# Where the row maxima of an attention are taken: a different share between the feed-forward and the heads, in a fused macaron block

## The chip, the cores and the metric

The kernel runs on one core of one Trainium2 chip. It is one launch that computes the whole block. Times are device microseconds (us) of the core. Five engines work beside each other, each through its own queue in order: TensorE (PE; its weight loads are PEld), VectorE (DVE), ScalarE (ACT), GpSimd (POOL) and SyncE (SP, which issues most of the DMAs). TensorE writes its results to PSUM, which has eight banks of 512 float32 values for each of 128 partitions.

## The reference

The input x has 4 sequences of 1024 rows of 512 values. A feed-forward, an attention and the same feed-forward again are added to it:

```python
x = x + 0.5 * ffn(layernorm(x), w_gate_up, w_proj)
x = x + attn(layernorm(x), Wq, bq, Wk, bk, Wv, bv, Wo, bo)
x = x + 0.5 * ffn(layernorm(x), w_gate_up, w_proj)

def ffn(x, w_gate_up, w_proj):            # weights made ternary in groups of 64, H = 2048
    gate, up = split(x @ quant(w_gate_up).T)
    h = silu(gate) * up
    return rms_norm(h) @ quant(w_proj).T

def attn(x, ...):                          # 32 query heads on 8 key heads, 16 wide
    Q, K, V = rope(x @ Wq.T + bq), rope(x @ Wk.T + bk), x @ Wv.T + bv
    w = softmax(Q @ K.T / 4)               # over 1024 keys
    return (w @ V) @ Wo.T + bo
```

## The kernel before

**Stages.** After the weights are quantised (together with the first two blocks of feed-forward), the program runs, for each of the four sequences b: a feed-forward stage (`FeedForward.run`, three blocks of 512 rows, so 48 units of 128 hidden values each), the heads of the attention (`Attention.run`), and a stage that ends this attention and projects the next sequence's Q, K and V. A last feed-forward stage of two blocks ends the kernel. In each of these loops the order of the instructions on every engine is the order in which the program writes them.

**A unit of the feed-forward.** `hidden` makes gate and up for 512 rows (16 matmuls of tile gu, L205), Silu on ScalarE, the product h on VectorE (L217), the square of h on POOL (sq, L225) summed into acc (L229). `project` (L245, tile po) follows two units later (LAG). At the end of a block, `sums` (L258, tile pq) adds the squares over the partitions with matmuls against ones, and `factors` turns them into half the inverse root: ms on VectorE (L273), inv on POOL (L98), half on VectorE (L277). `end` (x, L288) then scales po and adds it to x. At the end of a stage two units are left to project, tile by tile of 128 rows, and `factors` is called behind the second of the four tiles.

**The maxima.** The softmax needs the largest score of every row before its exps, since it subtracts it. The scores are therefore made twice. `maxima` makes them once in a form of two terms (matmul of tile sm, L1162: 128 rows against 512 keys, contracted over 64 of the 128 rows of the array, the lower half for even heads j and the upper half for odd ones) and VectorE reduces them to one column of pm (TENSOR_REDUCE, L1171). A sequence has 512 of them: 8 groups of 4 heads (G), each with 16 items (ITEMS: 8 row tiles, two halves of the keys). When a group, or from group 6 on half a group, is complete, `subtract_maxima` makes its negated maxima into rows: three short operations on VectorE (L1219 to L1223), a transposition on TensorE (pmT, L1201, in a bank of sm) and a copy (mrow, L1203). The rows of groups 0 to 2 go through DRAM (d_m, L1206) and come back on POOL's queue (`maxima_in`, L1242); those of later groups go by SP (L1213). They lie in even_rows or odd_rows.

**Where the maxima are taken.** `early` is called in each unit of the feed-forward and puts four maxima there, between two projections, as long as a share of EARLY is not yet reached and the unit is not one of a few left out. The rest comes in the heads.

**The heads.** 128 steps per sequence: for each group g and half of the queries qh, eight steps kc of 128 keys. One step makes the scores of two pairs of heads (`scores`, tile s, L1293, two matmuls a pair, one in each half of the array's rows), the exps (e, L1302, ScalarE), and, one step later, their product with the values (`weigh`, tile o, L1309, eight matmuls). The scores of a step are added to those of the step before in the same PSUM tile (the keys are stored as differences), so s of step kc must wait for the exps of kc - 1 of its pair; the maxima are subtracted once, in the first step of every eight, by two further matmuls a pair against the rows (L1293 too, `s<-even_rows,pick`). At the end of eight steps ScalarE copies o out (oT, L1318). PSUM holds two s tiles of two banks, three banks of sm (`bufs=3`) and one of o. Before the change a step takes three maxima, two behind the first pair's scores and one behind the second's, by a pattern of heads written out by hand; step 0 takes none. All matmuls of a step are written first, and the exps and reduces behind them.

**Key places.** `Places` holds the tiles of queries and keys for maxima ("m") and scores ("s") in four slots, and loads the next when an older one is over.

Of the kernel before, what the change touches and what calls it, by code (L numbers as in the profile page):

```python
# [10 lines left out]
F32 = mybir.dt.float32  # L11
BF16 = mybir.dt.bfloat16
F32R = mybir.dt.float32r
AF = mybir.ActivationFunctionType
# [8 lines left out]
HQ, HKV, HD = 32, 8, 16  # L23
G = HQ // HKV
# [13 lines left out]
def tile_macaron_block(  # L38
# [17 lines left out]
    nc = tc.nc  # L56
# [78 lines left out]
    class FeedForward:  # L135
# [176 lines left out]
        def chunks(self):  # L312
            last = len(self.order) - 1
            due, ends = [], []
            for n, (k, hc) in enumerate(self.order):
                if self.beside is not None and n > 0:
                    places.piece()
                parts, rest = self.hidden(k, hc)
                if ends:
                    self.end(*ends.pop(), [2, 3])  # L320
                due.append((k, hc, parts))
                behind = due.pop(0) if len(due) > self.LAG else None
                if behind is not None:
                    self.project(*behind, [0, 1])
                if n == last:
                    rest()
                if self.beside is not None:
                    share = (n - self.begin) / (last - 1 - self.begin)
                    self.beside(self.ps, share, n < last and (k == 0 or hc != self.LAG - 1))
                if behind is not None:  # L330
                    self.project(*behind, [2, 3])
                    if behind[1] == HC - 1:
                        half = self.factors(behind[0])
                        self.end(behind[0], half, [0, 1])
                        ends.append((behind[0], half))
                if n < last:
                    rest()
                if k + 1 < len(self.blocks) and 4 <= hc < 12 and hc % 2 == 0:
                    for turn in self.normalize(k + 1, [hc // 2 - 2], self.wp, self.ps, "gu"):
                        self.later.append((hc + 1, turn))  # L340
                for step in [step for step in self.later if step[0] == hc]:
                    self.later.remove(step)
                    step[1]()

            if len(self.accs[k]) > 1:
                self.sums(k, 0)
            for i in range(4):
                for behind in due:
                    self.project(*behind, [i])
                if i == 1:  # L350
                    half = self.factors(k)
            self.end(k, half)
            for _, step in self.later:
                step()
# [348 lines left out]
    class Places:  # L703
# [33 lines left out]
        def rest(self):  # L737
            while self.pieces:
                self.piece()
# [171 lines left out]
    class Attention:  # L911
# [17 lines left out]
        ITEMS = NT * 2  # L929
        TOTAL = HKV * ITEMS * G  # L930
        FIRST = 3
        EARLY = (3 * ITEMS - 4) * G

        def __init__(self, b):
            self.b = b
# [308 lines left out]
        def early(self, ps, share, more):  # L1244
# [12 lines left out]
            if self.turning:  # L1257
                self.turning.pop(0)()
            if more and sum(self.counts) + G <= min(share, 1.0) * self.EARLY:
                ends = [self.maxima(sum(self.counts) % G, ps, 4) for _ in range(G)]  # L1260
# [10 lines left out]
        def run(self, keep, wp, ps):  # L1271
            b = self.b
            o = None
            self.wp, self.ps = wp, ps
            self.odd_rows = wp.tile([P, T], F32R, tag="rows", name=f"odd_rows_{b}", bufs=1)

            sums = {}

            def scores(g, qh, kc, pair):

                name = f"{b}_{g}_{qh}_{kc}_{pair}"
                keys, queries = slice(kc * P, (kc + 1) * P), slice(qh * 512, (qh + 1) * 512)
                *q, k = places.at["s", b, g]
                if kc == 0:
                    sums[pair] = ps.tile([P, 2, 512], F32, tag="s", name=f"s_{b}_{g}_{qh}_{pair}", bufs=2)
                s = sums[pair]
                terms = [(k[:, keys], q[pair])]
                if kc == 0:
                    terms.append((pick[:, pair, :], self.mrows[g]))
                for n, (lhsT, rhs) in enumerate(terms):  # L1290
                    for e in range(2):
                        at = slice(e * PAIR, (e + 1) * PAIR)
                        nc.tensor.matmul(  # L1293
                            s[:, e, :],
                            lhsT=lhsT[at],
                            rhs=rhs[at, queries],
                            start=(kc == 0 and n == 0),
                            stop=(n == len(terms) - 1),
                            skip_group_check=True,
                        )  # L1300
                w = wp.tile([P, 2, 512], F32, tag="e", name=f"e_{name}", bufs=4)
                return w, lambda: nc.scalar.activation(w, s, AF.Exp, scale=1.0 / HD**0.5)  # L1302

            def weigh(g, qh, kc, es):
                nonlocal o
                if kc == 0:
                    o = ps.tile([P, 512], F32, tag="o", name=f"o_{b}_{g}_{qh}")
                for j in range(G):
                    nc.tensor.matmul(  # L1309
                        o[j * SLOT : (j + 1) * SLOT, :],  # L1310
                        lhsT=vs[:, kc, g, :],
                        rhs=es[j // 2][:, j % 2, :],
                        start=(kc == 0),
                        stop=(kc == NT - 1),
                    )
                if kc == NT - 1:
                    oT = wp.tile([P, 512], F32, tag="oT", name=f"oT_{b}_{g}_{qh}")
                    nc.scalar.copy(oT, o)  # L1318
                    nc.sync.dma_start(
                        self.d_o[g * G : (g + 1) * G, :, :, qh * 512 : (qh + 1) * 512].rearrange(  # L1320
                            "j r d t -> (j r d) t"
                        ),
                        oT,
                    )
                    if qh == NB - 1 and g % 2 == 1:
                        self.divide(g // 2, keep)
                        self.when = n


            pattern = [((0, 1), (2,)), ((3, 0), (1,)), ((2, 3), (0,)), ((1, 2), (3,))]  # L1330
            late = None
            places.load(("t2", b + 1) if b + 1 < B else ("out", B))
            for n in range(HKV * self.STEPS):
                g, qh, kc = n // self.STEPS, n // NT % NB, n % NT
                if n % self.STEPS == 4 and g > 0:
                    places.done(("s", b, g - 1))
                if n % self.STEPS > 0 and g + 1 < HKV and g + 1 in self.mT and g + 1 not in self.mrows:
                    self.maxima_in(g + 1)
                if self.after and n in (self.when + 7, self.when + 12, self.when + 15):
                    self.after.pop(0)()  # L1340
                if n == HKV * self.STEPS - 8 and b + 1 < B:
                    at[b + 1].rows_ahead(keep)
                turn = self.turning.pop(0) if self.turning else None
                sides = pattern[n % 4] if n > 0 else [(), ()]
                es, ends = {}, []
                for pair, heads in enumerate(sides):
                    es[pair], end = scores(g, qh, kc, pair)
                    ends.append(end)
                    for j in heads:
                        if self.counts[j] < HKV * self.ITEMS:  # L1350
                            ends.append(self.maxima(j, ps, 3))
                for end in ends:
                    end()
                if self.chores:
                    self.chores.pop(0)()
                if late is not None:
                    weigh(*late)
                if turn is not None:
                    turn()
                if n == 0:  # L1360
                    nc.gpsimd.memset(self.odd_rows.bitcast(F32), 0.0)
                late = g, qh, kc, es
            weigh(*late)
            places.done(("s", b, HKV - 2))
            places.done(("s", b, HKV - 1))
# [31 lines left out]
    for b in range(B):  # L1397

        n = 2 * NB - 1
# [73 lines left out]
```

## Time and profile before

| what | us |
|---|---|
| median of 3 runs (3166.61 to 3167.3) | 3166.78 |
| the profiled execution | 3165.26 |
| its span, first to last instruction | 3163.5 |
| TensorE busy | 3089.3 (98%) |
| VectorE busy | 2177.3 (69%) |
| ScalarE busy | 1757.6 (56%) |
| POOL busy | 915.2 (29%) |
| the 2048 reduces of the maxima (L1171) | 1281.8, 684 ns each |
| the 1024 exps (L1302) | 990.7, 1023 ns each |

The page comes from one profiled execution. A group line names line, engine and operation, then the tiles written and read, the count, the busy time and the mean of one. Behind a bar or in square brackets stands the idle time of the engine just before, and what ended it. Matmuls overlap, so their records are longer than the distance from one to the next; the chain of waits gives each only the time by which it moves the end. Its lines read: start, length, engine, tile and line, and how many instructions are merged.

### The profile page before, as it was taken

The page shows a single profiled execution, that of the slowest core. Times are in us where ns is not written, and L with a number is a line of the kernel's source. Part 1 is how long each engine was busy: PE and PEld are TensorE (multiplying, and loading weights), DVE is VectorE, ACT ScalarE, POOL GpSimd, SP SyncE. Part 2 cuts the span into 40 slices and gives each one's busy share as a digit, 9 for nine tenths or more (in the row PEclk, how much of TensorE's full clock was granted, in tenths as well). Part 3 has the DMA queues.
Part 4 walks back from the last instruction along what each step waited for, and adds up shares of the span by engine and source line. Part 5 has one row for each costly group of instructions (what it writes and reads, how often), then busy time and mean ns, then how long its engine had stood idle before and what let it go on. Part 6 is the DMA issues. An engine that isn't in the chain of part 4 may idle for free. (4 is left out here: it accounts for less than half of the span.)

```text
span 3163.5 us, 46228 instructions
## 1 busy us (share of the span) xinstructions
PE 3089.3 (98%) x16896; PEld 1953.4 (62%) x16896; DVE 2177.3 (69%) x3656; ACT 1757.6 (56%) x2346; POOL 915.2 (29%) x865
## 2 busy tenths in 40 slices
PE   5999999999999999999999999999999999999999
PEld 4777777733358777533387777333587776333787
DVE  7977666588846665788666665888556666887343
ACT  5752333389953333699913333899523335999343
POOL 2564333300034343200053333000243432000344
PEclk7999999999999999999999999999999999999999
DMA  3443322224334133143242222243341231342111
GB/s 110 156 136 97 92 62 80 60 87 107 115 89 127 55 94 109 48 125 95 89 121 85 88 81 62 76 111 117 88 131 56 77 97 62 94 126 66 40 60 41
DMA packets 231267, 285.52 MB, mean 90 GB/s; under 512 B 30048, under 2 KB 176736, under 8 KB 231040
## 3 DMA queue, kind: packets, MB, share of 16 engines
q1 hardware_dynamic: 224448, 272.32, 29.1%
q0 software_dynamic: 6592, 10.24, 1.4%
q8 instruction: 134, 2.20, 0.3%
q14 instruction: 93, 0.76, 0.1%
HBM read 215.35 MB, written 66.45 MB: 89 GB/s over the span
## 5 line engine op out<-in xcount | busy, mean ns | idle before, releaser
L1171 DVE TENSOR_REDUCE pm<-sm 128x1 f32<-128x512 f32 x2048 | 1281.8, 684 | 207.8 <-PE sm L1162 202.0
L1302 ACT ACTIVATE e<-s 128x1024 f32<-128x1024 f32 x1024 | 990.7, 1023 | 124.9 <-PE s L1293 121.7
L205 PE MATMUL gu<-xT,guT 128*128 128x512 f32 x1792 | 706.9, 394 | 4.3 <-DVE ql L1088 2.8
L205 PE MATMUL gu<-xL,guT 128*128 128x512 f32 x1792 | 700.8, 391 | 0.7 <-DVE xL L133 0.7
L1309 PE MATMUL o<-e,vs 128*32 128x512 f32 x4096 | 548.2, 604 | 0.0
L1162 PE MATMUL sm<-p_m,p_m 64*128 64x512 f32 x2048 | 491.9, 411 | 5.9 <-DVE h L217 5.9
L1293 PEld LDWEIGHTS s<-p_s,p_s 64*128 64x128 f32 x2048 | 193.8, 183 | 483.7 <-ACT e L1302 466.0
L1293 PE MATMUL s<-p_s,p_s 64*128 64x512 f32 x2048 | 467.7, 451 | 8.8 <-ACT e L1302 8.7
L225 POOL TENSOR_TENSOR sq<-h 128x512 f32<-128x512 f32 x210 | 218.7, 1042 | 713.9 <-DVE h L217 713.9
L217 DVE TENSOR_TENSOR h<-sg,gu 128x512 f32<-128x512 f32 x224 | 153.8, 686 | 375.4 <-PE gu L205 361.6
L215 ACT ACTIVATE sg<-gu 128x512 f32<-128x512 f32 x224 | 134.2, 599 | 479.5 <-PE gu L205 479.5
L205 PEld LDWEIGHTS gu<-xT,guT 128*128 128x128 f32 x1792 | 337.8, 188 | 78.8 <-ACT guT L94 3.2
L205 PEld LDWEIGHTS gu<-xL,guT 128*128 128x128 f32 x1792 | 337.8, 188 | 71.9 <-DVE xL L133 1.3
L245 PE MATMUL po<-w_pT,high 128*128 128x512 f32 x896 | 374.2, 418 | 0.9 <-DVE x L288 0.9
L245 PE MATMUL po<-w_pT,low 128*128 128x512 f32 x896 | 355.0, 396 | 0.0
L231 ACT CAST high<-h 128x512 fp32r<-128x512 f32 x224 | 139.0, 621 | 327.0 <-DVE h L217 320.6
L1162 PEld LDWEIGHTS sm<-p_m,p_m 64*128 64x128 f32 x2048 | 229.6, 185 | 83.3 <-DVE h L217 50.2
L229 POOL TENSOR_TENSOR acc<-acc,sq 128x512 f32<-128x512 f32 x205 | 275.9, 1346 | 16.1
L94 ACT CAST guT<-g 128x512 fp32r<-128x512 bf16 x448 | 274.9, 614 | 7.9 <-ACT guT L94 5.5
L245 PEld LDWEIGHTS po<-w_pT,high 128*128 128x128 f32 x896 | 168.2, 188 | 94.3 <-issue 56.4
L1309 PEld LDWEIGHTS o<-e,vs 128*32 128x32 f32 x4096 | 81.1, 108 | 183.3 <-issue 156.0
L233 DVE TENSOR_TENSOR low<-h,high 128x512 fp32r<-128x512 f32 x224 | 169.1, 755 | 35.4 <-ACT high L231 35.4
(159 smaller groups left out, 2869.3 us busy)
## 6 DMA issues: line engine op xcount, KB each, us to landing
g<-d_guT SPq DMA_DIRECT2D x448, 128.0 KB
p_m<-d_q SPq DMA_DIRECT2D x56, 512.0 KB
p_s<-d_q SPq DMA_DIRECT2D x56, 512.0 KB
d_o<-oT SPq DMA_DIRECT2D x64, 256.0 KB
p_m<-d_km SPq DMA_DIRECT2D x56, 256.0 KB
p_s<-d_ks SPq DMA_DIRECT2D x56, 256.0 KB
x<-in_L_attn_x_dram SPq DMA_DIRECT2D x32, 256.0 KB
w<-in_L_ffn_w_gate_up_dram SPq DMA_DIRECT2D x32, 256.0 KB
```

Of the source, the lines that this page charges most:

```text
L94: nc.scalar.copy(w, t)
L205: nc.tensor.matmul(pg, lhsT=self.weights[k, hc][part][:, c, :], rhs=xp[:, c, :], start=(c == 0 and low == 0), stop=(c == DC - 1 and low == 1),
L217: nc.vector.tensor_tensor(h, sg, gu[1], ALU.mult)
L225: nc.gpsimd.tensor_tensor(sq, h, h, ALU.mult)
L229: nc.gpsimd.tensor_tensor(acc, acc, sq, ALU.add)
L233: return (high, low), lambda: nc.vector.tensor_tensor(low, h, high.bitcast(F32), ALU.subtract)
L245: nc.tensor.matmul(self.pos[k][i], lhsT=h[:, i * P : (i + 1) * P], rhs=w_pT[hc], start=(hc == 0 and n == 0), stop=(hc == HC - 1 and n == 1),)
L1162: nc.tensor.matmul(s, lhsT=q[j // 2][at, i * P : (i + 1) * P], rhs=k[at, half * 512 : (half + 1) * 512], start=True, stop=True,)
L1171: nc.vector.tensor_reduce(pm[:, i, j, half : half + 1], s, AX.X, ALU.max)
L1293: nc.tensor.matmul(s[:, e, :], lhsT=lhsT[at], rhs=rhs[at, queries], start=(kc == 0 and n == 0), stop=(n == len(terms) - 1), skip_group_che ...
L1302: return w, lambda: nc.scalar.activation(w, s, AF.Exp, scale=1.0 / HD**0.5)
L1309: nc.tensor.matmul(o[j * SLOT : (j + 1) * SLOT, :], lhsT=vs[:, kc, g, :], rhs=es[j // 2][:, j % 2, :], start=(kc == 0), stop=(kc == NT - 1),)
```

## The change

Four edits. The last `factors` of a stage stands behind the first tile, not the second. EARLY falls from 44 times four maxima to 38. A first step of every eight (kc == 0) takes four maxima, the others three, and step 0 takes its four behind both pairs; the heads j simply follow each other, and each maximum is written with its reduce at once. In a first step the two matmuls that subtract the rows' maxima are written behind the first two maxima, directly ahead of the exp (in the second pair, directly behind its scores). Zeroing odd_rows moves from POOL in step 0 to VectorE in step 2, and `maxima_in` may run from the fourth step of a group on rather than from its second.

```diff
@@ FeedForward.chunks, the end of a stage
             for i in range(4):
                 for behind in due:
                     self.project(*behind, [i])
-                if i == 1:
+                if i == 0:
                     half = self.factors(k)
@@ Attention
-        EARLY = (3 * ITEMS - 4) * G
+        EARLY = (3 * ITEMS - 10) * G
@@ scores
                 terms = [(k[:, keys], q[pair])]
                 if kc == 0:
                     terms.append((pick[:, pair, :], self.mrows[g]))
-                for n, (lhsT, rhs) in enumerate(terms):
+
+                def product(n):
+                    lhsT, rhs = terms[n]
                     for e in range(2):
...
+                product(0)
                 w = wp.tile([P, 2, 512], F32, tag="e", name=f"e_{name}", bufs=4)
-                return w, lambda: nc.scalar.activation(w, s, AF.Exp, scale=1.0 / HD**0.5)
+
+                def end():
+                    if kc == 0:
+                        product(1)
+                    nc.scalar.activation(w, s, AF.Exp, scale=1.0 / HD**0.5)
+
+                return w, end
@@ the loop of steps
-            pattern = [((0, 1), (2,)), ((3, 0), (1,)), ((2, 3), (0,)), ((1, 2), (3,))]
...
-                if n % self.STEPS > 0 and g + 1 < HKV and g + 1 in self.mT and g + 1 not in self.mrows:
+                if n == 2:
+                    nc.vector.memset(self.odd_rows.bitcast(F32), 0.0)
+                if n % self.STEPS > 2 and g + 1 < HKV and g + 1 in self.mT and g + 1 not in self.mrows:
                     self.maxima_in(g + 1)
...
-                sides = pattern[n % 4] if n > 0 else [(), ()]
-                es, ends = {}, []
-                for pair, heads in enumerate(sides):
+                some = [sum(self.counts) + i for i in range(4 if kc == 0 else 3)]
+                some = [i % G for i in some if i < self.TOTAL]
+                es = {}
+                for pair in range(2):
                     es[pair], end = scores(g, qh, kc, pair)
-                    ends.append(end)
-                    for j in heads:
-                        if self.counts[j] < HKV * self.ITEMS:
-                            ends.append(self.maxima(j, ps, 3))
-                for end in ends:
-                    end()
+                    if pair == 1 or n == 0:
+                        end()
+                    for j in some[2 * pair : 2 * pair + 2] if n > 0 else some * pair:
+                        self.maxima(j, ps, 3)()
+                    if pair == 0 and n > 0:
+                        end()
...
-                if n == 0:
-                    nc.gpsimd.memset(self.odd_rows.bitcast(F32), 0.0)
```

## The prediction

> **What bounds the kernel now.** First the page's busy times: TensorE is busy 98% of the span, but so it is in both of the stages that the change touches, and pipelined matmuls make that number blunt. So I read, stage by stage, which wait ends last.
>
> ```profile
> PE 3089.3 (98%) x16896; PEld 1953.4 (62%) x16896; DVE 2177.3 (69%) x3656; ACT 1757.6 (56%) x2346; POOL 915.2 (29%) x865
> ```
>
> Then the busy time in windows, of the instructions on tile sm alone (PE, PEld, DVE). The first window is one feed-forward, the second the heads after it: how many maxima each really holds.
>
> ```profile
> 300.00:627.00 327.00, 31.63 (x168) 13.16 (x168) 104.32 (x168) 0.99 0.27 80
> 627.00:912.00 285.00, 91.26 (x344) 44.16 (x344) 216.13 (x344) 1.00 0.33 95
> ```
>
> 168 is 42 groups of four, so EARLY's 44 were never reached. Then the chain of waits in a feed-forward that holds maxima, and in the last one, which holds none.
>
> ```profile
> 2427.94 3.63 PE gu L205 x16
> 2431.57 0.94 PE po L245 x4
> 2432.50 0.66 PE sm L1162 x2
> 2433.16 1.13 PE po L245 x4
> 2434.29 3.63 PE gu L205 x16
> ...
> 3096.04 3.65 PE gu L205 x16
> 3099.69 1.87 PE po L245 x8
> 3101.56 3.65 PE gu L205 x16
> ```
>
> The reader is to see one engine alone: a unit lasts 6.35 with a group (2427.94 to 2434.29) and 5.52 without (3096.04 to 3101.56). A group costs 0.83 of TensorE there, and nothing else waits. Now the same view in the heads: one ordinary step, one first step of eight, and the beginning of the next.
>
> ```profile
> 2689.78 0.43 PE s L1293 x2
> 2690.20 0.24 PE sm L1162 x2
> 2690.44 0.24 PE s L1293 x2
> 2690.68 0.23 PE sm L1162
> 2690.91 1.00 PE o L1309 x8
> 2691.91 0.66 PE s L1293 x4
> 2692.56 0.23 PE sm L1162 x2
> 2692.80 0.46 PE s L1293 x4
> 2693.26 0.23 PE sm L1162
> 2693.49 0.99 PE o L1309 x8
> 2694.48 0.43 PE s L1293 x2
> ```
>
> Again TensorE alone: 2.13 for a step, 2.57 for a first step. Two sm (one in each half of the rows) take 0.23, and the single third takes 0.23 too: a fourth would fit beside it. Last, the timelines of VectorE, of the weight loads and of TensorE where a transposition has shifted the order of the three sm banks by one, so that a load must wait for a bank.
>
> ```profile
> 649.41 1.88 DVE L1171 TENSOR_REDUCE pm<-sm 128x1 f32<-128x512 f32 x3
> 651.34 0.18 PEld L1162 LDWEIGHTS sm<-p_m,p_m 64*128 64x128 f32 x1 [0.21 <-DVE pm L1171]
> 651.17 0.66 PE L1162 MATMUL sm<-p_m,p_m 64*128 64x512 f32 x2
> ```
>
> The last reduce ends at 651.29, the load starts 0.05 later, the pair's matmuls end at 651.83: 0.49 after the load. One reduce lasts 0.68 to 0.69, three take 1.88, so they follow each other by 0.60.
>
> **Four groups fewer in the feed-forward.** With EARLY 152 the share test and the skipped units let through 38 groups instead of 42. 4 groups x 4 stages x 0.83 = 13.3 us less. TensorE is the chain there, so all of it counts. The wait that a unit near the middle shows (the rows of group 0 on POOL's queue ahead of rstd, L1242 before L98: 2.82 of "issue" and 2.08 of DMA issues in the last such stage) moves from the unit after the 16th group at one even unit to another even unit, where the same rstd stands behind it: 0.
>
> **Where they go.** The heads take 360 instead of 344 maxima. Steps with maxima: 115 before (1 to 115), 115 after (0 to 114), so no step is gained or lost; the 16 extra are fourth ones, or step 0's.
>
> **The fourth maximum.** On TensorE itself it costs 0, beside the third. VectorE's four reduces, 4 x 0.60 = 2.40, fit in 2.57. But sm has three banks. In an ordinary step each bank has a whole step to come free; the fourth needs the bank of the first, of the same step. Time from the step's first product: s 0.43, the first two maxima 0.23, so the first ends at 0.66. Its reduce begins 0.04 later (646.85 to 646.88 in the timeline at a first step), lasts 0.69, the fourth's load starts 0.05 after that and its matmul ends 0.49 later: 1.93. Without a wait it would end with the third, at 0.43 + 5 x 0.23 = 1.58. So 0.35 of idle TensorE, and o, the next s, and everything else in its queue stand behind it. Steps 8, 16 to 112: 14 x 0.35 = 4.9 per stage. Bounds: 0 if the bank came free in time, 0.58 if the first maximum ended as late as before (behind the rows' product).
>
> [...]
>
> **The rows' product behind the first two maxima.** That puts exp of pair 0 0.23 later in first steps. ScalarE needs 16 x 0.92 + 0.48 = 15.2 of the 17.5 us of eight steps, and the bank wait gives it 0.35 more, so I take 0; if that cover goes (no bank wait), up to 0.23 x 16 = 3.7 per stage, since the copy of o (L1318) and the next step's two exps follow without a gap.
>
> **Step 0.** Before, step 1's first product ended at 2658.81, released by exp (2657.24 + 1.03). After, the rows' products end at 2657.68, the first two maxima at 2657.91, the fourth 0.04 + 0.69 + 0.05 + 0.49 = 1.27 later, the product 0.23 on: 2659.41, 0.60 late. In step 1 the second maximum needs the bank of step 0's third reduce (ends 2657.91 + 0.04 + 1.20 + 0.69 = 2659.84), so it ends 2660.38, 0.74 behind its place. Against that goes the 0.42 that step 1's pair loses today (0.65 for 0.23), which waits for banks that DVE x (L288) still reads. Together +0.9 (0.5 to 1.3). That the four find those banks free rests on the earlier factors below; without it some 1.7 us more.
>
> **Last sums behind the first tile.** The sums, ms, inv, half move forward by one tile's 0.93. At the end of the kernel x can then follow at once: the last x starts 0.9 earlier, still behind the last po: -0.9 us. In the four other stages only x on VectorE comes earlier, off TensorE's path: 0. If sq (POOL, 1.04) came later than the first tile, it would cost instead; it ends at 3151.38, the sums begin at 3152.9.
>
> **The rest.** Zeroing odd_rows moves from POOL (0.94) to VectorE, ahead of step 2's reduces. No row shows it there: between 0 and two reduces, 1.37. A bank has 2.13 - 1.27 = 0.86 to spare, so 0 to 0.5 per stage; nearest POOL's 0.94, I take 0.1, 0.3 in all.
>
> [...]
>
> Group 2 now ends in step 12, and its three short operations (0.22 + 0.19 + 0.21) run at once before a transposition whose load already waits 0.84 a time on a reduce (23.5 us in 28 waits); the shifted banks add to that: 0.4 per stage (0 to 1.0). Loads of later groups start 1 to 4 steps later on SP; the tightest, rows of group 5, land about one step before their use, so 0 (2 per stage if not).
>
> **Sum.** Heads 4 x (4.9 + 0.9 + 0.4) + 0.3 = 25.1; feed-forwards -13.3; end -0.9: **+10.9**. The profiled execution took 3165.26 (span 3163.5), 1.5 under the median of 3166.78; so 3176.2 against its own time, 3177.7 for the median. I say 3177.5. About 0.2%, 6.3 us, is what a measurement of this kernel tells from no change.
>
> **Rivals.**
> Faster: the fourth rides free. Place: the bank of the first maximum, steps 8 to 112. It decides if that bank is back 1.09 into the step instead of 1.44. For it: the single sm costs as much as two, VectorE idles 0.23 in each step. Against: the first maximum ends at 0.66 and a reduce lasts 0.69. Then -14.2 + 0 to 8 for the later exp: 3153 to 3161.
> About no change: the wait exists, but half is absorbed, because steps after it run faster (ScalarE holds some s products by 0.03 today) and step 0 costs little: 4 x 3.5 - 14.2, about 3166; 3162 to 3171.
> Slower still: the later exp also holds the next steps, or group 5's rows come late. +2 to 3 per stage on top: 3186 to 3198. Against it: ScalarE's 2.3 us of slack per eight.
>
> **How the numbers follow.** My sum 0.62: its low ends (4.9 + 0.5 + 0) give 3174, its high ends (4.9 + 1.3 + 1.0 + 0.5) 3183, and 3 more on either side for lags that I took from one place each: 3171 to 3186. Free ride 0.17, half absorbed 0.13, worse 0.08. The range leaves out the free ride and the far end of the worst case: 3162 to 3188. Same, 3160.4 to 3173.1, takes the half absorbed, 0.05 of my sum and 0.02 of the free ride: 0.20. Faster: the rest of the free ride, 0.15. Slower: 0.65.
>
> **What would show it.** Right: sm 152 and 360 in the two windows; first steps of some 2.92 in the chain, with a wait of the sm load for DVE pm (now 8 waits, 1.6 us) some 56 times or more; a heads stage 6 longer than its 279.8; a feed-forward 3.3 shorter. Wrong: first steps of 2.57 to 2.6 with four maxima, or a wait of s for ACT e in second and third steps instead.

## The result, and the profile after

| what | before | after |
|---|---|---|
| median of 6 runs, us | 3166.86 (3165.32 to 3168.71) | 3178.03 (3177.19 to 3182.47) |
| the profiled execution | 3165.26 | 3182.47 |
| its span | 3163.5 | 3180.7 |

The change makes the kernel slower: ratio 1.0039 (1.0026 to 1.0052), +11.2 us between the medians; the forecast was 3177.5. Four of the six runs after lie at 3177.2 to 3178.1 and two at 3182.3 and 3182.5; the profile is of one of these two.

The page again says next to nothing: TensorE is busy 98% in both.

```profile
PE 3107.5 (98%) x16896; PEld 1963.4 (62%) x16896; DVE 2186.4 (69%) x3660; ACT 1762.8 (55%) x2346; POOL 915.3 (29%) x861
```

Busy times in windows, of the instructions on tile sm alone (PE, PEld, DVE), a feed-forward and the heads after it: 152 and 360 maxima, so the change does what it says.

```profile
300.00:627.00 327.00, 28.73 (x152) 11.95 (x152) 94.40 (x152) 0.99 0.27 80
627.00:912.00 285.00, 97.79 (x360) 46.89 (x360) 225.50 (x360) 1.00 0.32 94
```

The chain of waits, a first step of eight in the heads after (start, length, what):

```profile
2685.51 0.43 PE s L1295 x2
2685.94 0.23 PE sm L1162 x2
2686.17 0.69 PE s L1295 x6
2686.87 0.59 PE sm L1162 x2
2687.45 1.00 PE o L1319 x8
2688.45 0.43 PE s L1295 x2
```

The step lasts 2.94 (2685.51 to 2688.45); before it lasted 2.57. The whole difference is in the second pair of sm: 0.59, where one sm took 0.23. Why it is late stands in the timelines of VectorE and of the weight loads:

```profile
2686.21 2.48 DVE L1171 TENSOR_REDUCE pm<-sm 128x1 f32<-128x512 f32 x4 [0.26 <-PE sm L1162]
2686.95 0.18 PEld L1162 LDWEIGHTS sm<-p_m,p_m 64*128 64x128 f32 x1 [0.29 <-DVE pm L1171]
```

The first two maxima end at 2686.17. The first reduce starts at 2686.21 and lasts some 0.69, so it ends at 2686.90; the fourth maximum's load starts at 2686.95, and its matmul ends at 2687.45. That is the predicted chain link by link: 0.66 into the step, + 0.04 + 0.69 + 0.05 + 0.49. Over the whole kernel the waits for it are (waiting and releasing instruction: us in total, times, longest):

```profile
PEld sm L1162 <- DVE pm L1171: 27.0, 82, 0.7
```

Before, this was 8 waits and 1.6 us; 56 waits or more were predicted. The sum of these waits is idle time of the weight loads, not time lost by TensorE; the price is read from the length of the steps.

Where the time went, by stage of the profiled executions (feed-forward: first to last unit's start; heads: first exp's start to last exp's end; worked out from the starts in the traces):

| stage | feed-forward before, after | heads before, after |
|---|---|---|
| 0 | 306.2, 305.1 | 279.7, 286.7 |
| 1 | 300.3, 297.0 | 279.9, 287.7 |
| 2 | 300.2, 296.7 | 279.7, 287.9 |
| 3 | 303.2, 296.6 | 279.7, 288.3 |

The feed-forwards give 14.5, the heads take 31.6, the end gives 0.9, and some 1.1 comes between and beside the stages: +17.2, the difference of the spans. The heads of stage 0 (+6.9) are the undisturbed ones. In the three others the granted clock falls to a half for 3.41 us right behind step 0, and they are 1.1 to 1.6 longer, 3.9 in all. Their first four steps are 1.2 longer each, 3.6 in all; the 0.4 left lies in stage 3, which is 0.4 to 0.5 longer in runs 4 and 6 too, with no drop in it. Without the 3.9 the span would be 3176.8, and the time about 3178.6, near the four other runs; those four have no trace here.

### The profile page after: what moved, and what is told of

Its sections match the earlier page's. It is cut to its first block, busy times and chain, and to the rows that moved or that the text cites. A ratio compares the mean times of both kernels' runs of the same rounds, so it can differ in the third digit from the quotient of the medians.

```text
span 3180.7 us, 46236 instructions
## 1 busy us (share of the span) xinstructions
PE 3107.5 (98%) x16896; PEld 1963.4 (62%) x16896; DVE 2186.4 (69%) x3660; ACT 1762.8 (55%) x2346; POOL 915.3 (29%) x861
## 5 line engine op out<-in xcount | busy, mean ns | idle before, releaser
L1162 PE MATMUL sm<-p_m,p_m 64*128 64x512 f32 x2048 | 505.5, 414 | 7.8 <-DVE h L217 5.1
L217 DVE TENSOR_TENSOR h<-sg,gu 128x512 f32<-128x512 f32 x224 | 153.9, 687 | 390.6 <-PE gu L205 376.7
```

What stands on the lines that cost most here:

```text
L217: nc.vector.tensor_tensor(h, sg, gu[1], ALU.mult)
L1162: nc.tensor.matmul(s, lhsT=q[j // 2][at, i * P : (i + 1) * P], rhs=k[at, half * 512 : (half + 1) * 512], start=True, stop=True,)
```

## The experiments

Theory: the fourth maximum waits for the bank of the first. Rivals: it rides free and the later exp is what costs; or an extra load costs by itself, wherever the bank is. The kernel before took 3166.61 beside runs 1 to 4, 3166.48 beside runs 5 to 8 and 3166.74 beside runs 9 and 10.

**1. Three maxima a step, none in step 0, 42 groups in the feed-forward; all else of the change stays.**

```diff
-        EARLY = (3 * ITEMS - 10) * G
+        EARLY = (3 * ITEMS - 4) * G
...
-                some = [sum(self.counts) + i for i in range(4 if kc == 0 else 3)]
+                some = [sum(self.counts) + i for i in range(3 if n > 0 else 0)]
```

> The changed kernel with three maxima in every step again (none in step 0) and 42 groups in the feed-forward, all its other edits kept: no fourth maximum, but the rows' product stays behind the first two maxima. Bank theory: first steps fall from 2.93 back to about 2.58 of TensorE, the loads of sm wait for VectorE's reduces hardly ever (under 15 times, against 82), and what is left over the kernel before is only the later exp, 0 to 0.23 per eight steps: 3166 to 3175 us, centre 3171. Rival (the later exp of the first steps is what costs, not the bank): the heads stay as long as in the changed kernel, some 7 per stage over the kernel before, and with the feed-forward's 13 us given back the time is 3188 to 3195.

3171.31 (3170.98 to 3173.75), ratio 1.0016 (1.0007 to 1.0026). The chain of waits of this run, a first step:

```profile
2750.16 0.43 PE s L1295 x2
2750.59 0.24 PE sm L1162 x2
2750.83 0.70 PE s L1295 x6
2751.54 0.23 PE sm L1162
2751.76 1.00 PE o L1319 x8
```

2.60 without the fourth, and the waits of sm for pm fall to 0.7 us in 4. So the 0.35 of a first step belongs to the fourth maximum alone. The heads are still 1.7 to 2.1 a stage longer than before: now the later exp costs something. By the ends of the matmuls the second pair's product of the third step (steps 10, 18 to 114), which must wait for the exp, takes 0.39 on the mean, 0.26 before: 0.13 each eight steps. With the bank wait in place it is 0.26. This is the cover that the prediction named, and its price when the cover goes (it gave up to 0.23).

**2. The kernel before, with the earlier `factors` alone.**

```diff
-                if i == 1:
+                if i == 0:
                     half = self.factors(k)
```

> The kernel before with one edit alone: the last factors of a stage behind the first tile. My sum: 0.9 us less at the end of the kernel, nothing in the four other stages, so 3166.0 (3165.0 to 3166.5), and in the trace the last x starts 0.9 nearer to the last po. Rival: the half that VectorE makes beside POOL's zeroing of odd_rows comes earlier too and step 1 of each heads stage (2.58) shortens by up to 0.4: 3164.3.

3164.62 (3163.14 to 3166.38), ratio 0.9993 (0.9984 to 1.0003): not told apart from no change by time, and below the range that I gave; the profiled span is 0.8 shorter. The rival named beside it is right in part: step 1 takes 2.57 for 2.73 (by the ends of its first products) in each of the four heads stages, 0.6 in all beside the 0.9 of the end. The end of the kernel shows it in the changed kernel too (chains of waits, the changed kernel): where sq ended, 2.71 of "issue" follow instead of 3.64, and the x in a row begins directly behind half.

```profile
3168.47 1.04 POOL sq L225
3169.51 2.71 issue
3172.22 1.07 POOLq L1479
3173.29 0.02 issue
3173.31 0.18 DVE half L277
```

**3. The rows' product at its old place, ahead of the first two maxima.**

```diff
                 product(0)
+                if kc == 0:
+                    product(1)
...
                 def end():
-                    if kc == 0:
-                        product(1)
```

> The changed kernel with one edit undone: in first steps the rows' product stands directly behind its pair's scores, as before, so the exp of pair 0 is 0.23 earlier but the first two maxima 0.23 later. Bank theory: the fourth waits 0.58 rather than 0.35, first steps take 3.17 of TensorE, 14 x 4 x 0.23 = 13 us more: 3191 (3187 to 3195). Rival (the later exp is the cost): faster than the changed kernel, 3165 to 3172.

3193.1 (3191.35 to 3195.26), ratio 1.0084 (1.0067 to 1.01). The chain of waits of this run now names the reduce itself:

```profile
2709.50 0.67 PE s L1295 x4
2710.16 0.27 PE sm L1162 x2
2710.43 0.69 DVE pm L1171
2711.13 0.04 issue
2711.17 0.49 PE sm L1162
```

The first maximum ends 0.23 later and so does the fourth: with the o behind it (0.99) a first step lasts 3.16, and the waits of sm for pm grow to 41.4 us in 88. This is the upper bound of the prediction, 0.58 a step, and it speaks against a load that costs the same wherever it stands. It also shows that moving the rows' product behind the maxima, the edit that I priced at nothing, is worth 13 us by the steps (14 x 4 x 0.23) and 15 by the medians, as soon as there is a fourth maximum. The profiled execution holds something else: in stage 3 TensorE waits 1.4 for the rows of group 5 at step 80 (in the chain a load of theirs issued at 2850.80 lands 6.11 later), a drop of the clock follows, and this stage takes 293.5 where the others take 289.9. In the changed kernel the last load of these rows is issued 4.1 before their first use, in the kernel before 5.95: the margin that the prediction priced at nothing is thinner, and here it was once used up.

**4. The first two maxima of a first step ahead of the scores of pair 0.**

```diff
+                ahead = kc == 0 and n > 0
+                for j in some[:2] if ahead else ():
+                    self.maxima(j, ps, 3)()
```

> The changed kernel with the first two maxima of a first step moved ahead of the first pair's scores, so that they end 0.23 earlier and nothing else moves: the exp of pair 0 stands where it does in the changed kernel. Bank theory: the fourth waits 0.12 rather than 0.35, first steps take 2.70 of TensorE; some 0.07 of the 0.23 per first step comes back as a wait of the third step's scores for the exp, which the bank wait hides today: 14 x 4 x 0.16 = 9 us less, 3169 (3165 to 3172). Rival (four reduces or the later exp are the cost): as the changed kernel, 3177 to 3179.

3169.97 (3168.76 to 3172.58), ratio 1.0012 (1.0002 to 1.0021). Chain of waits, a first step:

```profile
2710.70 0.43 PE sm L1162 x2
2711.14 0.92 PE s L1295 x8
2712.06 0.35 PE sm L1162 x2
2712.41 1.00 PE o L1319 x8
```

The first maximum now ends 0.43 into the step, 0.23 earlier, and 0.12 of the wait is left. The series is complete: with the first maximum's end moved by +0.23, 0 and -0.23, a first step lasts 3.16, 2.93 and 2.70, and 2.58 without a fourth. (The idle time of the sm loads is 56.3 us in 88 waits here, more than in run 3: it is not the price.) The time to a fourth is set by one bank's way round, 1.27 from the end of the first.

**5. Transpositions only in odd units of the feed-forward.**

```diff
-            if self.turning:
+            if self.turning and odd:
```

> The changed kernel with one more edit: in the feed-forward a transposition of maxima (and so the DMAs of group 0's rows on POOL's queue behind it) starts only in an odd unit, while rstd of the next block's rows stands on POOL in even units. My reading of the long units (9.65 and 7.53 in stage 0, 8.28 in the others, for 6.5 to 6.7): rstd waits behind those DMAs. Then they go: 4 us in stage 0, where the clock drops too, 1.6 in each other stage, 8.7 in all: 3169 (3167 to 3172). Rival: squares and sums on POOL take the wait over and the units stay as long: 3177 to 3179. Bank theory: first steps stay at 2.93.

3172.44 (3170.28 to 3176.57), ratio 1.0019 (1.0009 to 1.0029): 5.6 below the changed kernel's median, above the range that I gave. In the changed kernel the wait is where the prediction puts it, in another unit. POOL's timeline, stage 0:

```profile
460.49 0.80 POOL L1206 DMA_DIRECT2D d_m<-mrow  x1
463.43 2.08 POOL L1242 DMA_DIRECT2D even_rows<-d_m  x4 [2.15 <-DMA d_m<-mrow]
465.52 0.58 POOL L98 TENSOR_TENSOR rstd<-var,mhalf 128x1 f32<-128x1 f32 x1
```

rstd stands behind the rows' loads, which wait 2.15 for the rows on their way through DRAM, and TensorE waits for rstd by way of VectorE: in the chain of stage 3, rstd (L98) releases xn (L119), h (L217) stands behind xn, and the next load of sm waits for h. This unit lasts 8.3 (9.65 in stage 0, where the clock also drops), and 7.05 with transpositions in odd units, in all four stages. The feed-forwards lose 7.2 in all. But a drop of the clock now falls into the heads of stage 0 (287.8 against 286.6 in stages 1 and 2), and none into the other three.

**6. No maxima in step 0 (39 groups instead of 38).**

```diff
-                some = [sum(self.counts) + i for i in range(4 if kc == 0 else 3)]
+                some = [sum(self.counts) + i for i in range(0 if n == 0 else 4 if kc == 0 else 3)]
```

> The changed kernel with no maxima in step 0 and 39 groups in the feed-forward instead of 38. A group costs 0.83 a stage (3.3 in all); step 0's four cost, by the two traces, 1.2 a stage (first four steps 9.84 for 8.67), and in the profiled execution a drop of the granted clock to half in three of four stages, 1.2 each. So 3178 + 3.3 - 4.8 - (0 to 3.6): 3175 (3172.5 to 3177), and no drop of the clock in the first steps of the heads. Rival (step 0 is idle room and its four are free): 3181.

3174.89 (3173.66 to 3177.89), ratio 1.0027 (1.0017 to 1.0037), as expected, though not term by term: the 39th group costs the feed-forwards 1.2 rather than 3.3, since the long unit is 7.5 rather than 8.3 in three stages. The first four steps take 8.61 (1.82, 2.42, 2.13, 2.24) against 9.84 in stage 0 of the changed kernel and 8.67 before. The heads take 285.3 in three stages, 1.4 less than stage 0 of the changed kernel, and no drop of the clock stands at their beginning.

**7. The kernel before, with the earlier `factors` and the transpositions in odd units.** Two edits, those of runs 2 and 5, and none of the change's maxima.

> The kernel before with the factors behind the first tile and the transpositions in odd units only, nothing of the four maxima: 3164.6 less the long units of before (1.65 in three stages, 4.4 in the one whose clock drops): 3155 (3153 to 3159). Rival as for the odd unit: 3164 to 3166.

3154.19 (3153.82 to 3155.17), ratio 0.9961 (0.9947 to 0.9975): 12.3 below before and 24 below the changed kernel, the fastest of all. It keeps 168 and 344 maxima, the heads last 279.6, and the feed-forwards 304.4 and 298.7 to 298.9. Its chain of waits shows the unit with the transposition:

```profile
2472.03 0.11 PE pmT L1201
2472.14 0.87 PE sm L1162 x4
2473.02 1.12 PE po L245 x4
2474.14 0.44 PE pxn L130 x4
2474.58 3.66 PE gu L205 x16
```

The next unit starts on time: there is no "issue" and no POOL in it.

**8. Runs 4, 5 and 6 together, on the changed kernel.**

> The changed kernel with its first two maxima of a first step ahead of the scores, none in step 0, 39 groups, and transpositions in odd units. If the parts add: 3170 + 3.3 - 4.8 - 8.7 = 3159.8 (3157 to 3163). If the fourth maximum were worth its place this would beat the same without it (the kernel before with factors and odd units); by the bank theory it does not: its first steps still take 2.70 for 2.58, and the third step still waits for the exp.

3162.80 (3160.71 to 3167.27), ratio 0.9989 (0.998 to 0.9999), in the range but 3 above the sum of the parts. The best form of the change that I found; it doesn't reach run 7. The feed-forwards are 17.2 shorter than before in sum, the heads 3.4 to 4.0 longer in each stage.

**9. Zeroing odd_rows on POOL again (in step 2).**

```diff
-                    nc.vector.memset(self.odd_rows.bitcast(F32), 0.0)
+                    nc.gpsimd.memset(self.odd_rows.bitcast(F32), 0.0)
```

> The changed kernel with the zeroing of odd_rows on POOL again, still in step 2. In the first heads stage of the changed kernel the fourth step (step 3) is 2.49 long, and VectorE's memset (0.91) stands directly ahead of six reduces without a gap. If the memset is what costs there, step 3 falls to 2.13, the first four steps of that stage from 9.84 to 9.5, and that stage from 286.66 to 286.3. In the other three stages a drop of the granted clock in step 1 already leaves VectorE free before the memset, so nothing there. Time: 0 to 1 us below the changed kernel, 3177 to 3178. Rival, that step 3 is late because of step 0's bank waits alone: step 3 stays at 2.4 to 2.5.

3181.4 (3179.74 to 3188.09), ratio 1.0049 (1.0037 to 1.0062). Half a miss. Step 3 does fall to 2.12, so VectorE's memset did cost 0.35 there. But step 0 grows from 2.18 to 2.81 in every stage, so the first four steps are 0.3 longer. (In stage 3 of this trace the clock stays at a half for 6.83 us and they are another 3.0 longer.) The 0.3 is 1.1 of the 3.4 between the medians of this run and of the changed kernel; the rest is not placed. The timelines of POOL and VectorE of this run, ahead of step 0:

```profile
625.90 0.94 POOL L1347 MEMSET odd_rows<- 128x1024 f32 x1
625.97 0.90 DVE L277 TENSOR_SCALAR half<-inv 128x4 f32<-128x4 f32 x1 [1.15 <-POOL inv L98]
626.91 2.73 DVE L288 SCALAR_TENSOR_TENSOR x<-po,half,x 128x512 f32<-128x512 f32 x4
```

and the same instruction in the changed kernel:

```profile
626.70 0.17 DVE L277 TENSOR_SCALAR half<-inv 128x4 f32<-128x4 f32 x1 [1.15 <-POOL inv L98]
```

POOL's queue is free, so it zeroes long before step 2, right behind inv, and half on VectorE, 512 values, takes 0.90 instead of 0.17: it ends with the memset (626.87 and 626.84). The four x stand behind it, and step 0's maxima wait for the banks that x reads (loads of sm for x: 4.3 us in 8 waits, 1.9 in 4 in the changed kernel). Before has the same 0.90 in all four heads stages, each time beside POOL's memset of 0.94 (in stage 0 half at 627.95, the memset at 627.88), and 0.17 in the median of its 14 halves; there, step 0 had no maxima that could wait for it. What makes half last as long as the memset is not shown.

**10. Three maxima in step 0 instead of four.**

```diff
-                some = [sum(self.counts) + i for i in range(4 if kc == 0 else 3)]
+                some = [sum(self.counts) + i for i in range(4 if kc == 0 and n > 0 else 3)]
```

> The changed kernel with three maxima in step 0 instead of four (one more is then taken in step 115, which had none). If the bank wait of step 0's fourth maximum is what step 0 costs, step 0 falls from 2.18 to 1.83 (the row of before), step 1 stays at 2.6 to 3.05, since its pairs still wait for the banks of step 0's reduces, and the TensorE idle of the two steps falls by 0.35. If the drops of the granted clock at step 0 and 1 (3.41 us at half clock in three of four stages of the profiled run, 1.2 to 1.6 us each) come from the summed idle of those steps within one stretch of 3.41 us, they become rarer or go: then each heads stage is 0.4 to 2 shorter and the time is 3171 to 3176. Rival, that the drops depend only on where the stage falls in time: they stay in most stages, and the time is 3176 to 3178.

3174.19 (3173.36 to 3175.76), ratio 1.0024 (1.0015 to 1.0033). Step 0 falls to 1.83 and step 1 to 2.80 in all stages; the heads take 285.3 to 285.4 in three of them; no drop of the clock stands in the heads. One maximum in four of the 512 steps costs 3.8 us by the medians, 2.4 of it by the two steps themselves (4 x 0.6). Whether the missing drops are an effect of the change is not shown: see the last section.

## Why the prediction was right, and where it was not

**The fourth maximum**, 0.35 x 14 = 4.9 per stage: the mean over thirteen of the fourteen first steps in the trace is 2.935 against 2.580, 0.355, so 5.0. (The fourteenth, step 56, lasts 3.17; it also holds a transposition that stood in step 55 before.) Runs 1, 3 and 4 show the cause. The free ride falls: by it a first step would have stayed at 2.58. Half absorbed falls too; nothing behind the step gives it back. On TensorE two sm take 0.23 (2688.88 in the chain of the changed kernel), as one does (2689.34), so what decides is the bank.

**The later exp**, 0: right for the reason given. By the second pair's product of the third step it costs 0.13 an eight without the bank wait (run 1) and 0.08 with a third of it (run 4: 0.33), and nothing clear with all of it (0.26), so the rival that put 2 to 3 per stage on top falls.

**Step 0**, 0.9 (0.5 to 1.3): 0.82 in stage 0, as 2.18 + 3.05 against 1.83 + 2.58. Run 10 gives 0.6 of it to the fourth alone. What the sum did not hold are the three drops of the clock behind these steps.

**Memset**, mis-sized. I took 0.1 a stage; step 3 shows 0.35 in stage 0 (2.49 against 2.14), and run 10, without drops, shows 2.47 to 2.48 in all four. VectorE was already late by step 0's reduces: the timeline of stage 0 has seven reduces, the memset and six more with 0.16 between.

```profile
629.65 4.28 DVE L1171 TENSOR_REDUCE pm<-sm 128x1 f32<-128x512 f32 x7
634.09 0.91 DVE L1347 MEMSET odd_rows<- 128x1024 f32 x1 [0.16 <-issue]
634.92 3.61 DVE L1171 TENSOR_REDUCE pm<-sm 128x1 f32<-128x512 f32 x6
```

The slack of 0.86 that I set against it was that of an ordinary step, not of one behind a step that had used it: in runs 1 and 6, with the same memset and no maxima in step 0, step 3 takes 2.24, the 0.1 that I took. The instruction takes 0.91 on VectorE, near POOL's 0.94 from which I sized it. That the same move also takes 0.63 a stage off step 0 (run 9) I had not seen: I put free banks in step 0 down to the earlier factors alone.

**Group 2's three operations**, 0.4: step 13 lasts 2.97 against 2.42, 0.55 a stage.

**Loads of later groups**, 0: right in the trace of the changed kernel, where no wait for the rows of group 5 shows. That this could fail was said, and run 3 shows it once.

**Four groups fewer**, -13.3: stages 1 and 2 give 3.2 and 3.6, against 3.3 worked out. Stages 0 and 3 give 1.1 and 6.6, because a clock drop at the long unit stands in stage 3 before (that unit lasts 11.15 there, 8.3 to 8.5 in the others) and in stage 0 after (9.65, and 7.53 for the next). The wait itself moved to another even unit at its old price (8.3), as predicted: 0.

**End**, -0.9: the distance from the last unit's start to the end of the span is 17.94 before and 17.00 after. That the earlier factors are worth nothing in the other stages was not quite right: alone they shorten step 1 by 0.16 a stage (run 2).

In stage 0 the terms as measured are 5.0 + 0.82 + 0.35 + 0.55 = 6.7 of the 6.9; the rest isn't in one place. 4 x 6.9 - 14.5 - 0.9 + 1.1 = 13.3 on the profiled span of before gives 3176.8 again. The forecast of +10.9 missed some 2 of it, and the medians, 3166.86 and 3178.03, differ by +11.2: that the two agree to half a microsecond is partly luck.

## What to carry to other kernels

Before putting one more use of a rotating buffer into a step, write down when the first use ends, add the way round (wait, read, load, matmul: here 1.27), and compare that with the place where the new use would end; the busy share of the engine (TensorE: 98% before and after) says nothing on it. Take work out of a stage where it is on the chain, but price the stage that receives it at its tightest step, and move what shortens the way (here the rows' product) ahead of adding. When a stage shows one unit longer than the others, look there first: two small edits at that unit and at the end gave 12 us, and the whole change, with its 16 maxima moved in each stage, cost 11.

## What the runs showed of the hardware that was not expected

The granted clock falls in pieces of 3.41 us, and at the beginning of the heads it fell behind windows in which TensorE was idle for about a tenth of the time (0.36 to 0.38 of 3.41 in the three stages of the changed kernel). Busy times in windows of that length, the changed kernel (PE, PEld, DVE, ACT, POOL, then the granted clock):

```profile
628.96:632.37 3.41, 3.03 (x15) 1.36 (x11) 3.40 (x7) 2.98 (x4) 0.00 (x0) 1.00 0.00 0
2666.72:2670.13 3.41, 3.03 (x16) 1.16 (x13) 3.40 (x6) 3.00 (x4) 0.00 (x0) 1.00 0.62 229
2670.13:2673.55 3.42, 3.42 (x16) 1.34 (x15) 2.52 (x5) 1.42 (x2) 0.45 (x1) 0.50 0.00 0
```

The drop at 2670.13 follows a window in which TensorE was idle for 0.38. In run 10, with three maxima in step 0, a window over the same steps looks like this, and no drop follows; but it begins 0.44 ahead of the first exp, the one above 0.24 behind it:

```profile
2659.48:2662.89 3.41, 3.23 (x18) 1.61 (x14) 3.40 (x6) 2.97 (x4) 0.00 (x0) 1.00 0.82 304
2662.89:2666.31 3.42, 3.42 (x26) 1.23 (x26) 3.26 (x6) 2.60 (x3) 0.37 (x1) 1.00 0.00 0
```

The drops keep to one grid, wherever the stages begin: those at 256.91, 325.18, 468.54, 1311.63, 1990.88 and 2670.13 in the changed kernel's trace start 20, 42, 247, 199 and 199 windows of 3.413 apart. The windows ahead of the first three have TensorE busy for 1.18, 0.86 and 1.55, but those ahead of the three in the heads for 3.03 to 3.05: here 89% busy was followed by half clock. Nor does the busy share decide: on the same grid of the same trace, the window 915.68 to 919.09 has only 2.68 busy, and no drop follows.

What goes with the drops is where the grid meets the stage. Five traces take four maxima in step 0 (the changed kernel, runs 3, 4, 5 and 9), which makes 20 heads stages. In five of them a window of the grid begins 0.2 to 0.6 behind the first exp of the stage, and these five have a drop behind that window; in the fifteen others the nearest window begins 0.02 or more ahead of it, or 0.9 or more behind it, and none has one there. No stage of runs 6 and 10 has a window that begins in that place, so their traces cannot tell whether a shorter step 0 avoids the drop. One stage of run 1, with no maxima in step 0, has such a window and no drop. Why this place and not another is open.

A drop of 3.41 us behind step 0 cost 1.2 us in the first four steps (the changed kernel and run 5), one of 6.83 us cost 3.0 (run 9). Whether the drops are also what parts the runs at 3182 from those at 3178 is a guess, as only one of them has a trace.
